# A graph network on one core: the attention's alphas and sums moved from a tail into the second gather pass

## The chip, the core and the metric

The kernel runs on one NeuronCore of a Trainium2 chip. Time is device time of one execution in microseconds (us); a run's time is a little over the span of the profiled instructions. The core has a matrix engine (PE, with its weight loads shown as PEld), a vector engine (DVE), a scalar engine (ACT), GpSimd (POOL), which issues the indirect DMAs, and SyncE (SP), which issues most of the plain ones. Each engine runs its own instructions strictly in the order in which the program emits them, and waits on semaphores for the others.

## The reference, cut to what matters

There are N = 12500 nodes with 256 features, and E = 200000 edges, sorted by `dst`. Two graph convolutions with a residual are followed by one attention layer of H = 4 heads and C = 64 channels.

```python
def _gcn_conv(x, W, b, src, dst, n):
    h = x @ W
    deg = segment_sum(ones, dst)
    dinv = where(deg > 0, rsqrt(deg), 0.0)
    return segment_sum(h[src] * (dinv[src] * dinv[dst])[:, None], dst) + b

def _L1_gnn_ref(x, edge_index, weight, attn_l, attn_r):
    xt = (x @ weight).reshape(-1, heads, out_ch)
    row, col = edge_index
    alpha_l = einsum('ehd,hd->eh', xt[row], attn_l)
    alpha_r = einsum('ehd,hd->eh', xt[col], attn_r)
    alpha = softmax(leaky_relu(alpha_l + alpha_r, 0.01), axis=1)
    tmp = einsum('nh,nhd->nd', alpha[:n], xt[col[:n]])
    return broadcast_to(tmp[:, None, :], (n, heads, out_ch)).reshape(n, -1)

h = relu(layernorm(x));  x = x + gnn(h)        # pre, two _gcn_conv (self loops added), post
h = relu(layernorm(x));  x = x + _L1_gnn_ref(h)
```

Row i of the attention uses edge i, for i < n only. As the edges are sorted by `dst`, the first 12500 edges end in the first few hundred nodes, while their `src` lies anywhere. So edge i needs four numbers of any node (`alpha_l`) and a row of 260 numbers (256 of `xt`, four of `alpha_r`) of an early node.

## The kernel before, in words

**Tiles and chunks.** The nodes are NT = 98 tiles of 128; the edges are NCH = 112 chunks of J = 14 gathers of 128 edges, 1563 gathers in all. Each convolution is a pass over all gathers: POOL fetches the 128 source rows of a gather by an indirect DMA (L1397), DVE makes a chunk's one-hot matrices `fhot` of the edges' places (L1243), and PE multiplies the two and adds up in PSUM (`facc`, L1407). Rows are kept in DRAM as three bf16 parts whose sum is the f32 value, so a gather takes three bf16 matmuls. Rows land in rotating buffers `fgot`; in pass 2 there are 4 buffers of `ONE = 9` gathers.

**Stages.** Preparation; pass 1, whose first 56 gathers take raw rows of x, the next 336 f32 rows of `ftable1`, the remaining 1171 bf16 parts (`split_rows` makes the parts, three gathers apart, while the f32 gathers run); pass 2, 1563 gathers of bf16 parts; and an attention tail.

**The order by hand.** `convolve` emits the whole program for a pass, gather by gather. Work of a finished node tile is queued with `at(t + o, step)` and emitted when the loop has reached gather t + o. A chunk's sums are copied by ACT (`fsums`, L1288), transposed by PE eight gathers later (`fturn`, L1208) and added on DVE thirteen gathers later (`buf`, L1305); the tile that this completes has its steps 6 to 34 gathers on. In pass 2 these are `finish2`'s d (`fpz`), e, f (`fpo`), g (the new x, stored to `kept_x` by SP), h, i (`fpt`), k, q (`fpx`: the product with the attention's weights) and r. A tile completes about every 16 gathers. Before its first gather, `convolve` turns the first rows' own sums (self loops) on PE and calls `ready(0)`.

**What belongs to the attention.** In step r ACT copies tile w's four `alpha_l` numbers and stores them to two tables in DRAM, `table_l` and `table_e`, and for the first XW = 9 tiles the 260-number rows to `table_r`. During pass 2 `set_up` loads `src` and `dst` to all partitions and makes the one-hots `hot_l` and `hot_t`, and the rows of the first 14 edge tiles (`fxe`) are multiplied early. After pass 2 the tail goes through the 98 edge tiles in groups of G = 7. For each tile POOL gathers `alpha_l` by `src` (`fal`, L1751) and PE fetches the end's row by a one-hot product (`fends`, L1741), which ACT copies (`fxg`, L1743). For each group DVE forms the scores, the softmax (with ACT's Exp), the weighted sum over heads (`near`, `far`, `some`, `more`, `fmix`), and adds it to `kept_x` (`fxr`, loaded by SP) to give `fres`, which SP stores. `missing` adds the last three tiles' alphas for the first 14 edge tiles.

**A second path.** If the edges don't fit the kernel's assumptions, a flag `bad` starts a general path after all this; here it is not taken.

Of the kernel before, what the change touches and what calls it, by code (L numbers as in the profile page):

```python
# [8 lines left out]
F32 = mybir.dt.float32  # L9
# [404 lines left out]
def fast_path(  # L414
# [64 lines left out]
    assert AC * J == NT and AC * CE <= E and XW < NT  # L479
    table_r = dram.tile([XW * P, DR], F32, name="table_r")  # L480
    table_l = dram.tile([NT * P, H], F32, name="table_l")

    LW = 3
    table_e = dram.tile([NT * P, H], F32, name="table_e")
# [18 lines left out]
    base_b = const.tile([P, NCH], F32, name="base_b")  # L503
    row_i = const.tile([P, AC], I32, name="row_i")
# [88 lines left out]
    with tc.tile_pool(name="fprep", bufs=1) as prep:  # L593
# [233 lines left out]
        with tc.tile_pool(name="fpsum", bufs=2, space=PSUM) as psum, \  # L827
# [227 lines left out]
            wide = prep.tile([NCH, P], F32, name="wide")  # L1055
            nc.vector.tensor_copy(wide, base.to_broadcast([NCH, P]))
# [7 lines left out]
            nc.tensor.matmul(fk[:, 2, :NCH], wide, ident[:NCH, :NCH], start=True, stop=True)  # L1064
# [7 lines left out]
            for f in after:  # L1072
                f()
            after = [raw_block(ends, m, psum.tile([P, 4 * P], F32, name="ft"), j0)
                     for j0 in (8, 12)]
            nc.vector.tensor_copy(base_b, fk[:, 2, :NCH])
            nc.vector.tensor_scalar(row_i, base_b[:, :AC], lane, float(XW * P - 1), op0=ALU.add,
                                    op1=ALU.min)
# [16 lines left out]
    def check_chunks(work, psum):  # L1095
# [20 lines left out]
        kept = work.tile([1, 1], F32, name="n_kept", bufs=1)  # L1116
        nc.vector.tensor_reduce(kept, pt[:1, 2, :NCH], AX.X, ALU.add)
        nc.vector.tensor_add(kept, kept, counted)
        nc.vector.tensor_scalar(bad_row, kept, -1.0, float(NCH + 1), op0=ALU.mult, op1=ALU.add)
# [12 lines left out]
    def load_late(pool):  # L1132

        nc.scalar.dma_start(roots, root_t)
        for t, w in ((wb, w2), (wo, w_post), (wg[:, :, :D], w_gat)):
            nc.scalar.dma_start(t, w.rearrange("(k p) n -> p k n", p=P))
        nc.scalar.dma_start(b2c, b2.rearrange("(k p) -> p k", p=P))
        nc.scalar.dma_start(bob, b_post.partition_broadcast(P))
        attn = []
        for a in (attn_r, attn_l):  # L1140
            ar = pool.tile([P, D], F32, name="far", bufs=2)
            nc.scalar.dma_start(ar, a.rearrange("h c -> (h c)").partition_broadcast(P))
            attn.append(ar)
        return attn

    def late_weights(pool, attn):

        for i, ar in enumerate(attn):
            for k in range(KC):
                prod = pool.tile([P, H, C], F32, name="fprod", bufs=1)  # L1150
                nc.vector.tensor_mul(prod.rearrange("p h c -> p (h c)"), wg[:, k, :D], ar)
                nc.vector.tensor_reduce(wg[:, k, D + i * H:D + (i + 1) * H], prod, AX.X,
                                        ALU.add)

    def convolve(ep, table, stride, width, ahead, with_sum, psum, prepare, finish, parts, since,
                 lacking=False, raw=(), rows_p=None, behind=None):
# [35 lines left out]

        def new_buf():
# [24 lines left out]
        for n0 in range(0, BW, P):  # L1218
            v, n = {}, min(P, BW - n0)
            new_turned(v)  # L1220
            turn_sums(load_rows(n0, n), 0, v)
            nc.vector.tensor_copy(state["buf"][0][:, :, n0:n0 + n], v["pt"][:, :KC, :n])
            if with_sum:
                nc.vector.tensor_copy(state["buf"][1][:, n0:n0 + n], v["ps"][:, 0, :n])
# [6 lines left out]
        ready(0)  # L1231


        const_p = psum.tile([P, P if with_sum else P + D], F32, name="iota_p", bufs=1)
        iota_p = const_p[:, :P]
        nc.vector.tensor_copy(iota_p, iota_w)
        if not with_sum:
            state["bias"] = const_p[:, P:]
            nc.vector.tensor_copy(state["bias"], bob)

# [21 lines left out]
        def new_rows_of():  # L1262
            if with_sum:
                return new_got()
            return rows_p.tile([P, ONE, 3 * stride], BF16, name="fgot", bufs=ahead)

        def late_sums():
# [3 lines left out]
            froms = new_rows_of().rearrange("p j d -> p (j d)")[:, :J * D]  # L1271
            froms = froms.rearrange("p (j d) -> p j d", d=D)
            assert stride == TW * P and D == TW * P
            for i in range(TW):
                one_hots(froms[:, :, i * P:(i + 1) * P], from_0[:, i, :])
            px = psum.tile([P, KC, P], F32, name="fpt", bufs=1)
# [100 lines left out]
        for t, (c, j) in enumerate(tiles):  # L1377
# [4 lines left out]
            if many == 1:  # L1382
                if j == 0:
                    gots = (raw + [spare])[c] if raw and c <= len(raw) else new_rows_of()
                got = gots[:, j, :]
            else:
                i = (t - since * J) % ONE
                if i == 0:
                    gots = new_rows_of()
                    if since:  # L1390
                        gots = gots.rearrange("p j d -> p (j d)").bitcast(BF16)
                        gots = gots[:, :ONE * 3 * stride].rearrange("p (j d) -> p j d", j=ONE)
                got = gots[:, i, :]
# [16 lines left out]
            if some and j == nj[c] - 1:  # L1410
                for i in range(TW):
                    nc.tensor.matmul(acc, late[0][:, i, :], late[1][i], start=False,
                                     stop=(i == TW - 1))
            if j == nj[c] - 1:
# [3 lines left out]
            if behind:  # L1418
                behind(t)
            run(t)  # L1420
        run()
# [51 lines left out]
    def split_rows(pool, psum):  # L1473
        rows = {}

        def load(w):
            rows[w] = pool.tile([P, D1], F32, name="frow", bufs=4)
            nc.sync.dma_start(rows[w], table1[w * P:(w + 1) * P, :])

        def step(t):  # L1480
# [3 lines left out]
            if k < NT:  # L1484
                load(k)
            if k >= 2:
                p = psum.tile([P, 4, P], F32, name="fpt", bufs=1)
                p = p.rearrange("p a b -> p (a b)")[:, :D1]
                b = pool.tile([P, 3, D1], BF16, name="frow_p", bufs=3)
# [3 lines left out]
                to_parts(p, b, parts1, k - 2)  # L1493

# [5 lines left out]
    assert 3 * D1 * ONE <= 2 * D1 * J and J * D <= 3 * D * ONE  # L1500
# [341 lines left out]
```

## Time and profile before

| | us |
|---|---|
| three runs of the kernel, median | 4876.28 |
| the same, lowest and highest | 4865.6, 4886.07 |
| the profiled execution's own time | 4877.83 |
| its span | 4875.9 |
| preparation, to the first gather from the f32 table's chunks | 0 to 135 |
| pass 1, f32 rows | 135 to 675 |
| pass 1, bf16 parts, with the wait for pass 2's first rows | 675 to 2378 |
| pass 2, first to last gather | 2378 to 4626 |
| what is left of pass 2 after its last gather | 4626 to 4669 |
| the attention's tail | 4669 to 4876 |

The stages are read from the start times of POOL's gathers (L1397 and L1751). POOL is in the row of the gathers' issue nearly all the time: one issue takes 949 ns (2720 of them, 2580.2 us), with 0.30 us between two. DVE and ACT are busy 28% and 13% of the span, PE 54%; the mean granted clock of PE is 0.68 of full speed.

In the tail, POOL's 98 gathers, PE's products, ACT's copies and DVE's mixing follow each other group by group; there is no other work beside them.

### The profile page before, as it was taken

The page shows a single profiled execution, that of the slowest core. Times are in us where ns is not written, and L with a number is a line of the kernel's source. Part 1 is how long each engine was busy: PE and PEld are TensorE (multiplying, and loading weights), DVE is VectorE, ACT ScalarE, POOL GpSimd, SP SyncE. Part 2 cuts the span into 40 slices and gives each one's busy share as a digit, 9 for nine tenths or more (in the row PEclk, how much of TensorE's full clock was granted, in tenths as well). Part 3 has the DMA queues.
Part 4 walks back from the last instruction along what each step waited for, and adds up shares of the span by engine and source line. Part 5 has one row for each costly group of instructions (what it writes and reads, how often), then busy time and mean ns, then how long its engine had stood idle before and what let it go on. Part 6 is the DMA issues. An engine that isn't in the chain of part 4 may idle for free. (4 is left out here: it accounts for less than half of the span.)

```text
span 4875.9 us, 38956 instructions
## 1 busy us (share of the span) xinstructions
PE 2648.6 (54%) x13306; PEld 1780.7 (37%) x13306; DVE 1387.0 (28%) x3009; ACT 614.7 (13%) x1625; POOL 3109.7 (64%) x3299
## 2 busy tenths in 40 slices
PE   5756555555555555555545555545455555545553
PEld 4534433233233333333333334333333343434341
DVE  7445532112122222222222222222222222212236
ACT  5212210000000000000001100010111101101011
POOL 7566646666666666666566666666666666666643
PEclk7766666666666666666666667666676766767766
DMA  8566655555555555555556666565566666656635
GB/s 269 147 178 184 191 157 154 159 158 161 163 156 161 158 162 157 160 157 163 147 157 177 162 159 155 158 161 151 154 159 160 157 156 156 163 153 158 159 110 155
DMA packets 413533, 787.28 MB, mean 161 GB/s; under 512 B 101005, under 2 KB 267172, under 8 KB 413324
## 3 DMA queue, kind: packets, MB, share of 16 engines
q0 software_dynamic: 197264, 594.53, 46.8%
q1 hardware_dynamic: 170214, 173.89, 11.4%
q10 hardware_dynamic: 45846, 16.27, 1.3%
q8 instruction: 107, 1.75, 0.2%
q14 instruction: 102, 0.84, 0.1%
HBM read 692.31 MB, written 92.05 MB: 161 GB/s over the span
## 5 line engine op out<-in xcount | busy, mean ns | idle before, releaser
L1397 POOL DMA_INDIRECT fgot<-parts,fsrc_t x2720 | 2580.2, 949 | 1372.9 <-issue 783.2
L1407 PE MATMUL facc<-fgot,fhot 128*128 128x256 bf16 (+2 forms) x8986 | 1743.4, 335 | 1152.0 <-issue 1105.8
L1407 PEld LDWEIGHTS <-fhot 128*128 128x128 bf16 x8202 | 902.3, 113 | 1593.5 <-issue 1399.0
L1243 DVE TENSOR_TENSOR fhot<-iota_p,to_t 128x1792 bf16<-128x1792 f32 (+1 forms) x224 | 449.2, 2005 | 8.0 <-remote 8.0
L1397 POOL DMA_INDIRECT fgot<-ftable,fsrc_t x336 | 318.8, 949 | 184.0 <-issue 104.2
L1468 DVE TENSOR_TENSOR fpo<-fpo,fparts 128x256 f32<-128x256 f32 x97 | 41.8, 431 | 922.8 <-ACT fo L1454 704.4
L1549 DVE SCALAR_TENSOR_TENSOR fy<-rb,fb2c,fpz 128x128 f32<-128x128 f32 x194 | 58.7, 344 | 850.4 <-remote 677.6
L1305 DVE TENSOR_TENSOR buf<-buf,fturn 128x256 f32 x224 | 94.4, 421 | 699.1 <-remote 510.0
L1558 PE MATMUL fpo<-fwo,fz 128*128 128x256 f32 x388 | 149.2, 523 | 200.1 <-ACT fz L1552 126.8
L1288 ACT ACTIVATE fsums<-facc 128x257 f32<-128x257 f32 (+1 forms) x224 | 85.2, 380 | 1326.9 <-remote 1122.2
L1563 DVE SCALAR_TENSOR_TENSOR fx<-fpo,fdinv,fxb 128x256 f32<-128x256 f32 x97 | 46.9, 483 | 643.4 <-remote 366.9
L1407 PEld LDWEIGHTS facc<-fgot,fhot 128*128 128x128 f32 x784 | 179.4, 237 | 131.2 <-issue 98.1
L1445 PE MATMUL fpo<-wf,buf 128*128 128x256 f32 x388 | 149.2, 496 | 125.5 <-issue 82.3
L1542 PE MATMUL fpz<-buf,fwb 128*128 128x128 f32 x776 | 137.4, 327 | 117.6 <-issue 99.5
L1558 PEld LDWEIGHTS fpo<-fwo,fz 128*128 128x128 f32 x388 | 91.3, 261 | 233.1 <-ACT fz L1552 142.6
L1208 PE MATMUL fturn<-fident,fsums 128*128 128x128 f32 x448 | 118.4, 348 | 100.2 <-issue 52.4
L1542 PEld LDWEIGHTS fpz<-buf,fwb 128*128 128x128 f32 x776 | 121.7, 236 | 127.4 <-issue 104.4
L1208 PE MATMUL fturn<-fident,self 128*128 128x128 f32 x396 | 106.6, 352 | 82.5 <-issue 46.7
L1445 PEld LDWEIGHTS fpo<-wf,buf 128*128 128x128 f32 x388 | 87.9, 248 | 161.5 <-issue 99.1
L1597 PE MATMUL fpx<-fwg,ht 128*128 128x4 f32 (+1 forms) x388 | 69.2, 286 | 129.9 <-ACT ht L1588 99.0
L1751 POOL DMA_INDIRECT fal<-table_l,fsrc_t x84 | 80.5, 958 | 69.3 <-DVE fs L1758 44.6
L1208 PEld LDWEIGHTS fturn<-fident,fsums 128*128 128x128 f32 x448 | 70.7, 177 | 144.8 <-issue 75.4
(284 smaller groups left out, 2272.8 us busy)
## 6 DMA issues: line engine op xcount, KB each, us to landing
fgot<-parts,fsrc_t POOLq DMA_INDIRECT x2720
parts<-frow_p SPq DMA_DIRECT2D x98, 195.0 KB
parts<-fparts SPq DMA_DIRECT2D x98, 192.0 KB
frow<-ftable SPq DMA_DIRECT2D x98, 130.0 KB
self<-ftable SPq DMA_DIRECT2D x99, 128.0 KB
self<-ftable SPq DMA_DIRECT2D x97, 130.0 KB
ftable<-fo ACTq DMA_DIRECT2D x98, 128.0 KB
kept_x<-fx SPq DMA_DIRECT2D x98, 128.0 KB
```

The source lines that it names most:

```text
L1208: nc.tensor.transpose(v["pt"][:, i * KC + k, :], rows[:, k * P:(k + 1) * P], ident)
L1243: nc.vector.tensor_tensor(h, iota_p[:, None, :].to_broadcast([P, n, P]), to[:, :, None].to_broadcast([P, n, P]), ALU.is_equal)
L1288: nc.scalar.activation(sb, acc, AF.Copy)
L1305: nc.vector.tensor_add(b, b, v["pt"][:, :KC, :])
L1397: nc.gpsimd.indirect_dma_start(out=got, out_offset=None, in_=rows_of[:(NT - TW) * P, :] if some else rows_of[:], in_offset=bass.IndirectOf ...
L1407: nc.tensor.matmul(acc, hots[c][:, j, :], got[:, i * stride:i * stride + width], start=(j == 0 and i == 0), stop=(j == nj[c] - 1 and i == ...
L1445: nc.tensor.matmul(po, buf[:, k, :P], wf[:, k, :], start=(k == 0), stop=False)
L1542: nc.tensor.matmul(pz[:, m, :], wb[:, k, m * P:(m + 1) * P], buf[:, k, :P], start=(k == 0), stop=(k == KC - 1))
L1549: nc.vector.scalar_tensor_tensor(y[:, m, :], v["root"], b2c[:, m:m + 1], v["pz"][:, m, :], op0=ALU.mult, op1=ALU.add)
L1558: nc.tensor.matmul(po, v["z"][:, m, :], wo[:, m, :], start=(m == 0), stop=(m == KC - 1))
L1597: nc.tensor.matmul(px, v["ht"][:, k, :], wg[:, k, d0:], start=(k == 0), stop=(k == KC - 1))
L1751: nc.gpsimd.indirect_dma_start(out=al[:, i, :], out_offset=None, in_=(table_l if c else table_e)[:], in_offset=bass.IndirectOffsetOnAxis(a ...
```

## The change

The attention's work is moved into pass 2. `convolve` takes a list `behind` of items. `feed(t)`, called once a gather, takes the first item if its condition holds (so many tiles finished) and the space of the item before has passed, and queues the item's parts one gather apart. The items, in order (the number is the space in gathers):

- `begin`, `picked` (4): small tables.
- `ends_of_tile` (14 times 7): an SP DMA with an address read from memory loads, for each edge tile, the 32 consecutive early nodes that its edges can end in; partition 4n + h holds head h of the n-th of them (65 numbers).
- `alpha_r` (14 groups, 4 each): a row of the edges' ends, broadcast by DMA to all partitions (229 KB, bf16); a one-hot on DVE (128 x 896); 7 f32 products; an ACT copy into `al`.
- `late_hots` (4 times 6) and `late_ends` (16 times 4), for *late* edges, those whose `src` lies in tile LATE = 84 or after: transposed one-hots and rows of 260 numbers, stored to DRAM.
- `alpha_l` for stages of source tiles (0,18), (18,36), (36,54), (54,72): once a stage's tiles are done, the four numbers per node are split into three bf16 parts (`l_of_stage`), and for each of 14 groups (4 gathers each) a row of `src` mod 128 is loaded by SP (229 KB), DVE makes a bf16 one-hot, PE multiplies (21 bf16 products of 72 columns), and DVE masks by the source tile (`mask`), multiplies 128 x 504 in PSUM, reduces, and adds to `al`.
- The last stage (72,84) and the rest are 14 `group` items, 10 gathers apart (the last 17): the `alpha_l` part, the softmax in two parts, the shares split into three bf16 parts, turned by one product, spread over 128 partitions by 7 products (`pick`), multiplied by the one-hot of the ends (`weigh`), and 7 f32 products with `ends` that give the mixed rows. `add_mix` adds them to `kept_x` and stores the group; the last two groups wait in `mixes`.
- `rest` (three): the same sum for the last 14 tiles, once their x is done.

Late edges have a wrong row after this, which is replaced: `list_late`, spread over pass 1, lists up to 16 times 128 late edges with their fields (7 products for each of 14 groups, and small steps). After the last gather, POOL fetches their rows of `kept_x` (16 gathers, 10 of them earlier), PE makes 16 products with the late tiles' alphas, DVE the softmax and the sums, in rounds of 2, 2, 4, 4, 4 of the 16, and POOL scatters the 16 groups of rows to `out`.

Removed are the tail, both alpha tables, `own_rows`, `set_up`, and the early ends. Further: PSUM banks of pass 2 are shared out anew (`fX`, `fY`, two `behind`); gather blocks of pass 2 are 3 buffers of 14 in place of 4 of 9; `frow` and `frow_p` have two buffers each in place of 4 and 3, and the load comes after the use; in pass 1 the first rows' sums (`begin_sums`) and `ready(0)` come after chunk 0's products.

```diff
@@ convolve
+        free_at = [0]
+        def feed(t):
+            if behind and t >= free_at[0] and behind[0][0]():
+                _, space, parts = behind.pop(0)
+                for i, part in enumerate(parts):
+                    if part:
+                        at(t + i, lambda _, part=part: part())
+                free_at[0] = t + space
...
-        ready(0)
+        if not with_sum:
+            begin_sums()
+            ready(0)
...
-            return rows_p.tile([P, ONE, 3 * stride], BF16, name="fgot", bufs=ahead)
+            return rows_p.tile([P, J, 3 * stride], BF16, name="fgot", bufs=ahead)
...
+            if with_sum and t == J - 1:
+                begin_sums()
+                ready(0)
...
-            if behind:
-                behind(t)
+            if every:
+                every(t)
+            feed(t)
             run(t)
@@ finish2, step r
-            nc.scalar.activation(xa[:, d0:], v["px"], AF.Copy)
-            nc.scalar.dma_start(table_l[w * P:(w + 1) * P, :], xa[:, DR:])
-            if w < NT - LW:
-                nc.scalar.dma_start(table_e[w * P:(w + 1) * P, :], xa[:, DR:])
...
+            nc.scalar.activation(l_all[:, w, :], v["px"][:, DR - d0:], AF.Copy)
+            mark("w", w)
@@ attend
+        def alpha_l(s, b):
...
+            def load():
+                v["row"] = row_of(lo_rows, b, "lo_all", 1)
+            def equal():
+                v["h"] = new_hot().bitcast(BF16)[:, :HE]
+                nc.vector.scalar_tensor_tensor(v["h"], v["row"], 0.0,
+                                               banks["lane"].to_broadcast([P, HE]),
+                                               op0=ALU.subtract, op1=ALU.is_equal)
+            def product():
+                p = bank()[:, :G * nw * H]
+                for j in range(G):
+                    for i in range(3):
+                        nc.tensor.matmul(p[:, j * nw * H:(j + 1) * nw * H],
+                                         v["h"][:, j * P:(j + 1) * P], l_parts[s][:, i, :],
+                                         start=(i == 0), stop=(i == 2))
...
+            def taken():
...
+                nc.vector.tensor_tensor(v["p"], v["p"],
+                                        mask[:, :, :, None].to_broadcast([P, G, nw, H]), ALU.mult)
...
+            return [load, None, equal, product, taken]
...
+        def group(b):
...
+            return [load, None, equal, product, taken, lambda: v["soft"][0](),
+                    lambda: v["soft"][1](), split, turn, turned, over(0, 4), weigh(0, 4), over(4, G),
+                    weigh(4, G), mix, end]
@@ after pass 2
-        for g in range(len(groups) + 2):
-            if g < len(groups):
-                keep(g)
-                ends_of(g)
-            if g >= 2:
-                mix(g - 2)
+        for k in range(KL):
+            nc.tensor.matmul(z[k // 8][:, k % 8, :, :], sets["hot"][:, k * P:(k + 1) * P],
+                             l_all[:, LATE:, :], start=True, stop=True)
...
+        for n in [2, 2] + [4] * ((KL - 4) // 4):
...
+            nc.vector.tensor_mul(near, heads[:, k, :, :C],
+                                 share[:, k, :, None].to_broadcast([P, n, H, C]))
...
+            for i in range(k0, k0 + n):
+                nc.gpsimd.indirect_dma_start(
+                    out=out[:], out_offset=bass.IndirectOffsetOnAxis(ap=late_i[:, 0, i:i + 1],
+                                                                     axis=0),
+                    in_=sets["x"][:, i, :], in_offset=None)
```

The emitted order puts the parts of pass 2 here, in gathers of that pass: `alpha_r` 317 to 369, `late_hots` 372 to 390, `late_ends` 396 to 456, `alpha_l` from 463 with four stages of 56 gathers each, the groups 1408 to 1553 of 1563. In pass 1 `list_late` lies between gathers 376 and 490.

## The prediction

> **What bounds the kernel now.** I read the page's totals first, then a table of stages, then the tail's groups, then who waits in pass 2. The totals and the two costliest groups:
>
> ```profile
> PE 2648.6 (54%) x13306; PEld 1780.7 (37%) x13306; DVE 1387.0 (28%) x3009; ACT 614.7 (13%) x1625; POOL 3109.7 (64%) x3299
> ...
> L1397 POOL DMA_INDIRECT fgot<-parts,fsrc_t x2720 | 2580.2, 949 | 1372.9 <-issue 783.2
> L1407 PE MATMUL facc<-fgot,fhot 128*128 128x256 bf16 (+2 forms) x8986 | 1743.4, 335 | 1152.0 <-issue 1105.8
> ```
>
> A gather costs POOL 0.949 us and 0.30 of issue, 1.25. The table of stages (length; busy us and count of PE, PEld, DVE, ACT, POOL; clock; DMA share; GB/s) gives what a gather really takes:
>
> ```profile
> 135.00:231.00 96.00, 66.46 (x280) 51.52 (x281) 45.47 (x146) 30.90 (x66) 53.42 (x56) 0.72 0.46 127
> ...
> 3000.00:3600.00 600.00, 316.75 (x1825) 230.14 (x1825) 136.42 (x295) 62.53 (x172) 392.84 (x415) 0.70 0.60 156
> ...
> 4626.00:4669.00 43.00, 27.39 (x161) 22.12 (x159) 15.62 (x49) 10.82 (x30) 6.20 (x7) 0.81 0.23 65
> 4669.00:4876.00 207.00, 82.24 (x254) 50.13 (x254) 108.12 (x202) 35.45 (x101) 94.18 (x98) 0.62 0.48 148
> ```
>
> Pass 2 takes 600/415 = 1.446 us per gather: 0.19 over POOL's own. The first stage, where PE (69%) and DVE (47%) also work on raw rows, takes 96/56 = 1.714. The last 207 us hold nothing but the attention, with no engine over 52%. Where POOL's 0.19 go shows in its waits from 2378 to 4626 us (total, times, longest):
>
> ```profile
> POOL fgot L1397 <- issue: 445.1, 1460, 0.3
> POOL fgot L1397 <- remote: 245.2, 73, 4.9
> POOL fgot L1397 <- PE facc L1407: 28.9, 7, 7.2
> ```
>
> Some 90 pauses of 2 to 5 us for a buffer that PE must free. So POOL sets the pace, and PE and what PE waits for set its pauses. What PE waits for from 3000 to 3600 us:
>
> ```profile
> PE facc L1407 <- issue: 104.0, 122, 2.5
> PE fpz L1542 <- issue: 38.8, 15, 8.7
> PE fpo L1558 <- ACT fz L1552: 32.0, 7, 10.6
> PE fpx L1597 <- ACT ht L1588: 22.7, 4, 12.7
> ```
>
> When PE does wait at a step between engines, it is long (32.0/7 = 4.6 us), but only in 7 of some 26 tiles.
>
> **What the change removes.** The sum goes against the profiled execution's own 4877.8 us, 1.5 over the median of the runs.
>
> The tail, 4668.5 to 4875.9: -207.4. In its place after the last alpha:
> 16 products. The nearest row is `lacks` on the chain of waits, 42 records in 8.77 us, two records a product, 0.42 each: 6.7. Mask and reduce, four DVE operations of 448 elements by `more` (0.59): 2.4, and 0.2 for an add. Softmax: six small operations at 0.19, and 1.85 for ACT's Exp and back (DVE's idle time before L1763, 27.7 us in 15): 3.0. Three operations over 16 x 256 elements, 12288 in all, by `near`:
>
> ```profile
> L1751 POOL DMA_INDIRECT fal<-table_l,fsrc_t x84 | 80.5, 958 | 69.3 <-DVE fs L1758 44.6 <-issue 24.7
> ...
> L1774 DVE TENSOR_TENSOR near<-fxg,share 128x896 f32<-128x896 f32 (+2 forms) x13 | 13.2, 1015 | 0.4
> ...
> L1779 DVE TENSOR_TENSOR more<-near,far 128x448 f32<-128x448 f32 (+2 forms) x15 | 8.9, 592 | 0.0
> ```
>
> 1.015 us for 896 gives 13.9. The last four scatters: 4 x 1.25 = 5.0, and 5 to land. No scatter is in the trace; by a gather's issue it is 1.25, at most the 2.30 of the raw rows' gathers in preparation, which would make 16 of them 42 us and the tail some 65; at best all hides but the last, 28. I take 36.2. The `rest` items (DVE 1792, 1024 and 768 elements, about 4 us) lie in the 43 us after the last gather, where DVE is busy 15.6; without that cover they cost 4. Net -171.2 (bounds -179 to -142).
>
> Pass 1's start: PE turns self rows from 138.8 to 146.4 while chunk 0's rows wait for it; put behind the products they leave the path, but the one-hots and raw scaling stay. -5 (0 to -7). `own_rows`, `hot_l`, `hot_t` and 14 early products (6.7 us of PE, 24.1 us of idle time before them): -5 (0 to -8). The two stores of alphas per tile were ACT issues off the path: 0.
>
> **What it adds.** An `alpha_l` item, every 4 gathers (5.8 us at the present pace): DVE one-hot of 896 elements by `fhot` (2.02 us for 1792) 1.0, mask 0.2, multiply and reduce of 504 by `more` 0.66 each, add 0.2: 2.7 us, or 47% on top of 23%. PE: 21 products; successive `fpx` records of 4 columns start 0.11 us apart and gathers' of 256 columns 0.11 or 0.21 by the clock, so 2.3 to 4.4 us on top of 53%. That fits only narrowly, and it is of the first stage's kind (DVE 47%, PE 69%, the next matrix waiting for DVE), which pays 1.714 - 1.446 = 0.27 a gather. Below stands 0: gathers in pass 1 and pass 2 keep 1.43 to 1.45 however many tile steps lie among them, since POOL's pauses have room behind them. Queued behind PE's wait for a one-hot are the gathers' products, and behind these the buffer that POOL needs. I take 0.20, nearer the upper row because DVE's share is the higher: 224 x 0.20 = +45 (0 to +60).
>
> The 14 groups, 147 gathers: 10 gathers hold about 43 products and 8 us of DVE of 14.5, with five returns from PE to DVE or ACT. I take the whole 0.27: +40 (0 to +80, twice the row).
>
> `alpha_r` and the late items, 144 gathers with about a quarter of that work: 0.07 each, +10 (0 to +39). `list_late`, 114 gathers in pass 1, 14 times 2 us of DVE and 7 short products: 0.08 each, +9 (0 to +31). The upper ends are 0.27.
>
> SP: 98 broadcasts of 229 KB, 22 MB. The nearest row, `to_all` of 896 KB, was used 6 us after issue at 2494.4; here two gathers (2.9 us) lie between load and use, and four between two uses of the one buffer. DMA is 60% busy, so I take 0; SP's queue also holds `rb`, `fxb` and self loads, needed tiles later. If a load comes 1 us late each time, 56 us; that is in the rival below. Blocks of 14: 42 gathers in flight in place of 36; gain or loss under 20, I take 0.
>
> The Trainium skill speaks against more DVE work beside gathers: SBUF — State Buffer, section "SBUF: two separate sides", says that GpSimd cannot write descriptors while DVE holds the shared port in a two-port mode. The rows do not show it: a gather takes 0.949 us in the mean and 0.958 in the tail with DVE at 52%. If all of some 270 us of added DVE work held the port, the sum would be some 270 higher; by the rows it is not changed.
>
> Sum: 4877.8 - 171.2 - 5 - 5 + 45 + 40 + 10 + 9 = 4800.6; against the median, 4799.
>
> **The rivals.** *The cover holds wholly.* The added work disappears in PE's idle 47% and in POOL's pauses: 4877.8 - 181.2 - 1.5 = 4695. For: the pace of a gather is the same in the f32 stage, pass 1 and pass 2. Against: 0.27 in the first stage.
>
> *Lock-step, slower.* In `alpha_l` DVE's next one-hot stands behind `taken`, which needs PE's product; PE's next product needs that one-hot. If each return takes the 4.6 us of PE's waits for ACT, an item takes 1.7 (mask to add) + 1.0 + 2.3 + 4.6 = 9.6 against 5.8: +3.8 x 56 = 213 in place of 45, so 4967. It decides as soon as the additions pass 181 + 24, that is 1.8 us more per item than I take. For: DVE shows waits for PE of up to 18 us. Against: only 7 of 26 tiles wait, and in the raw chunks four such returns in 14 gathers cost 4 to 6 us.
>
> *The tail does not shrink as said.* The last group ends ten gathers before the end, but PE works up to 36 gathers behind POOL; if the last three groups and the late rows are still due when the gathers stop, each group costs what it cost in the tail (207/14 = 15): 4799 + 45 = 4844.
>
> **How the numbers follow.** Forecast 0.38 (own range 4755 to 4845), wholly covered 0.22, lock-step 0.28, long tail 0.12. About 0.5%, 24 us, is what a measurement of this kernel can tell from no change: same is 4852 to 4901. Faster: 0.35 of the forecast's, 0.22 and 0.06 of the long tail's, 0.63; same: 0.03 + 0.06 + 0.03 of a lock-step in half of the items, 0.12; slower: the rest of the lock-step, 0.25. The range goes from the covered case, less the unknown ends, 4685, to 4960, just short of the full lock-step; 0.07 are left below and 0.13 above.
>
> **What would show it.** Right: the time per gather is 1.6 to 1.75 in the gathers 463 to 519, 641 to 697, 935 to 991, 1229 to 1285 and 1408 to 1553, and 1.45 elsewhere; pauses still end on PE; 75 to 85 us after the last gather. Wrong: 1.45 everywhere (covered); over 2.2 there, with PE waiting for `hot_s` and DVE for `behind` (lock-step); gathers' own duration over 1 us (the port); over 110 us after the last gather (long tail); POOL ending on DMA `lo_all` (the loads).

## The result, and the profile after

The changed kernel takes 5085.66 us (median of four runs, 5071.06 to 5091.46) against 4881.17 for the kernel before (four runs): ratio 1.0418, 95% interval 1.0398 to 1.0437. It is 4.2% slower; 4799 had been forecast. In the last seven runs of this study the kernel before takes 4150 us, also on a chip on which it had taken 4878 earlier; these runs are kept apart below, and the result above belongs to the condition with some 4880.

The page of the changed kernel, the lines that answer to those of before:

```profile
PE 2786.0 (55%) x15210; PEld 1956.4 (39%) x15210; DVE 1627.4 (32%) x3575; ACT 623.8 (12%) x1643; POOL 3029.6 (60%) x3226
...
L1419 POOL DMA_INDIRECT fgot<-parts,fsrc_t x2720 | 2570.9, 945 | 1682.8 <-issue 788.1
L1429 PE MATMUL facc<-fgot,fhot 128*128 128x256 bf16 (+2 forms) x8986 | 1776.6, 343 | 967.6 <-issue 922.5
```

A gather's issue takes as long as before (945 ns, 949 before); POOL's idle time in front of the gathers has grown by 310 us. The stages are read from the starts of POOL's gathers. Pass 2 begins at 2381.2 (2378.6 before), issues its last gather at 4930.7, and the span ends at 5069.3. So pass 2's gathers take 2549.5 us, 302.5 more than before; what lies behind them takes 138.6 in place of 250.4; pass 1 and what lies before it, 2.6 more. The sum, +193.3, is the whole difference of the two spans. Of the 302.5, 13 us lie in the gathers 0 to 310 of the pass, 56 in 310 to 463, 23 in 463 to 530, 128 in 530 to 1405 and 82 in 1405 to 1562. A table of stretches (length; busy us and count of PE, PEld, DVE, ACT, POOL; clock; DMA share; GB/s):

```profile
2837.00:3002.00 165.00, 104.82 (x555) 89.61 (x554) 44.75 (x86) 13.89 (x48) 81.20 (x86) 0.60 0.54 148
...
3410.00:3513.00 103.00, 50.44 (x380) 36.22 (x380) 35.95 (x72) 6.28 (x18) 56.72 (x60) 0.64 0.52 149
3615.00:3744.00 129.00, 66.92 (x373) 49.80 (x371) 25.96 (x59) 12.32 (x34) 85.37 (x92) 0.66 0.54 156
...
4752.00:4931.00 179.00, 106.06 (x736) 86.10 (x735) 89.05 (x211) 28.51 (x60) 77.44 (x83) 0.67 0.67 209
4931.00:5069.00 138.00, 49.79 (x323) 41.37 (x322) 54.15 (x127) 19.13 (x44) 31.29 (x33) 0.67 0.35 105
```

POOL's count tells the pace: `alpha_r` 165/86 = 1.92 us a gather, an `alpha_l` stage 103/60 = 1.72, plain gathers 129/92 = 1.40, the groups 179/83 = 2.16. DMA is busy 67% at most. What POOL waits for in the whole pass (total, times, longest):

```profile
POOL fgot L1419 <- issue: 451.6, 1463, 4.4
POOL fgot L1419 <- PE facc L1429: 450.6, 44, 15.9
POOL fgot L1419 <- remote: 141.9, 46, 5.3
```

By the starts of its gathers POOL pauses 99 times in pass 2 (97 before), but the pauses are twice as long: 597 us beyond the usual 1.25 in place of 291, and those that end on PE's gather products reach 15.9. All 99 stand at the first gather of a block of 14, and 91 of the 97 before at the first of a block of 9: there POOL needs a buffer that PE has to free. One more thing is seen in the timeline of a group (start, length, engine, line, tile, count; in brackets the idle time before and what ended it):

```profile
4947.89 0.70 PE L2066 MATMUL behind<-l_parts,hot_s 128*128 128x48 bf16 x21 [0.66 <-DVE hot_s L2058]
...
4948.76 1.70 PE L2147 MATMUL behind<-ends_all,weights 128*128 128x64 f32 x14
...
4954.33 0.52 DVE L2076 TENSOR_TENSOR behind<-behind,mask 128x336 f32<-128x336 f32 x1 [4.70 <-remote]
...
4961.45 0.54 ACT L2155 ACTIVATE mixes<-behind 128x448 f32<-128x448 f32 x1 [11.86 <-remote]
```

PE's 21 products end at 4948.6 by their records and DVE, idle from 4949.6, starts on them at 4954.3; the mixed rows end at 4950.5 and ACT, idle, starts at 4961.5. POOL issues eleven of the late edges' 16 gathers (not ten, as said of the change) back to back from 4945.7 to 4959.1. In the first case DVE itself is not late: the trace has PE's semaphore rise at 4954.30, 0.03 us before DVE starts. The kernel before shows the same: of 261 instructions of DVE and ACT in pass 2 that wait for PE and stood idle when PE's record of the product ended, half start more than 1.1 us behind that end, a quarter more than 5.7.

After the last gather: 67.9 us until the 16 products with the late alphas begin at 4998.6 (the last groups and tiles), 13.7 to the first scatter, 44.6 for the 16 scatters, and 12.4 to the end.

```profile
5046.71 0.97 POOL L2298 DMA_INDIRECT out_dram<-fgot,late_i  x1 [2.23 <-DMA out_dram<-fgot,late_i]
5049.39 0.97 POOL L2298 DMA_INDIRECT out_dram<-fgot,late_i  x1 [1.71 <-DMA out_dram<-fgot,late_i]
```

Each scatter waits for the landing of the one before.

### The profile page after: what moved, and what is told of

Same layout as the page of the kernel before. It is cut to its first block, busy times and chain, and to the rows that moved or that the text cites. A ratio compares the mean times of both kernels' runs of the same rounds, so it can differ in the third digit from the quotient of the medians.

```text
span 5069.3 us, 43794 instructions
## 1 busy us (share of the span) xinstructions
PE 2786.0 (55%) x15210; PEld 1956.4 (39%) x15210; DVE 1627.4 (32%) x3575; ACT 623.8 (12%) x1643; POOL 3029.6 (60%) x3226
## 5 line engine op out<-in xcount | busy, mean ns | idle before, releaser
L1429 PE MATMUL facc<-fgot,fhot 128*128 128x256 bf16 (+2 forms) x8986 | 1776.6, 343 | 967.6 <-issue 922.5
L1825 PE MATMUL fX<-buf,fwb 128*128 128x128 f32 x776 | 164.3, 361 | 138.6 <-issue 115.6
L1832 DVE SCALAR_TENSOR_TENSOR fy<-rb,fb2c,fX 128x128 f32<-128x128 f32 x194 | 58.6, 344 | 547.3 <-remote 477.3
L1846 DVE SCALAR_TENSOR_TENSOR fx<-fX,fdinv,fxb 128x256 f32<-128x256 f32 x97 | 46.8, 483 | 582.6 <-remote 274.2
L2066 PE MATMUL behind<-l_parts,hot_s 128*128 128x72 bf16 (+1 forms) x1470 | 91.0, 223 | 237.1 <-issue 152.1
L1825 PEld LDWEIGHTS fX<-buf,fwb 128*128 128x128 f32 x776 | 143.7, 268 | 148.1 <-issue 119.8
L1841 PE MATMUL fX<-fwo,fz 128*128 128x256 f32 x388 | 131.2, 471 | 113.1 <-issue 69.4
L2066 PEld LDWEIGHTS <-hot_s 128*128 128x128 bf16 x1470 | 73.6, 116 | 262.8 <-issue 165.1
L1880 PE MATMUL fY<-fwg,ht 128*128 128x4 f32 (+1 forms) x388 | 75.8, 304 | 130.6 <-ACT ht L1872 88.8
L1841 PEld LDWEIGHTS fX<-fwo,fz 128*128 128x128 f32 x388 | 85.3, 244 | 133.2 <-issue 73.3
```

Of the source, the lines that this page charges most:

```text
L1429: nc.tensor.matmul(acc, hots[c][:, j, :], got[:, i * stride:i * stride + width], start=(j == 0 and i == 0), stop=(j == nj[c] - 1 and i == ...
L1825: nc.tensor.matmul(pz[:, m, :], wb[:, k, m * P:(m + 1) * P], buf[:, k, :P], start=(k == 0), stop=(k == KC - 1))
L1832: nc.vector.scalar_tensor_tensor(y[:, m, :], v["root"], b2c[:, m:m + 1], v["pz"][:, m, :], op0=ALU.mult, op1=ALU.add)
L1841: nc.tensor.matmul(po, v["z"][:, m, :], wo[:, m, :], start=(m == 0), stop=(m == KC - 1))
L1880: nc.tensor.matmul(px, v["ht"][:, k, :], wg[:, k, d0:], start=(k == 0), stop=(k == KC - 1))
L2066: nc.tensor.matmul(p[:, j * nw * H:(j + 1) * nw * H], v["h"][:, j * P:(j + 1) * P], l_parts[s][:, i, :], start=(i == 0), stop=(i == 2))
```

## The experiments

Runs are single unless said otherwise, each with the kernel before on the same chip; one run is good to some 0.3%. The changed kernel by its ratio would take 5103 us beside a before of 4898.7, and 5080 to 5082 beside 4876 to 4878.

**Is it the round trip?** Three edits to the `alpha_l` items, and one that stretches the groups.

```diff
# no_alpha_l: the four stages' items left out
-                items.append((when("w", STAGES[s][1]), 4, alpha_l(s, b)))
# no_return: products made, never read
+                items.append((when("w", STAGES[s][1]), 4, alpha_l(s, b)[:4]))
# late_taken: `taken` three gathers later, behind the next item's one-hot
-            return [load, None, equal, product, taken]
+            return [load, None, equal, product, None, None, None, taken]
# groups_wide: two gathers between steps that wait for another engine
-            return [load, None, equal, product, taken, ...
+            return [load, None, both, product, None, None, None, taken, ...
```

> The 56 alpha_l items of the first four stages are left out (their alphas are missing in the result). By the trace of the changed kernel the gathers in and just behind these four windows take some 150 us more than 1.44 us each. Both theories expect a time 130 to 165 us under the changed kernel's 5086, so 4920 to 4955; a time above 5000 would say that the loss in these windows is only moved to another place.

> The alpha_l items keep their row load, one-hot and 21 products, but no one reads the products (the three DVE operations and the add of `taken` are left out). Round-trip theory (DVE's next one-hot stands behind `taken`, which waits for PE's result to be noticed, and PE stands until that one-hot): 100 to 140 us gained, 4945 to 4985. Work theory (the added products, one-hots and loads cost this much in any order): 50 us or less gained, above 5035.

> All work is kept; only `taken` of an alpha_l item is emitted seven gathers after the load in place of four, so the next item's one-hot no longer stands behind it. Round-trip theory: 70 to 120 us gained, 4965 to 5015, and an item takes 6 to 6.5 us in place of 8.3. Work theory: no change beyond 20 us, 5065 to 5105.

> All work is kept; the steps of a last-stage group stand two gathers apart where one engine waits for another (25 gathers long in place of 15, still 10 between groups). In the changed kernel a group takes 22 us where 10 gathers should take 14.4. Round-trip theory: 40 to 80 us gained in the gathers, 10 to 20 lost after the last gather, so 5010 to 5060. Work theory: nothing gained, 5085 to 5110.

Beside 4898.7 us: no_alpha_l 5017.6, no_return 5102.3, late_taken 5095.2, groups_wide 5116.0. The items cost 86 us, less than the 128 that the trace shows in the gathers 530 to 1405, and less than the 130 to 165 expected: by the expectation's own mark of 5000, part of the loss is elsewhere. In that run the gathers 530 to 1405, with no item among them, still take 38 us more than in the kernel before, 5 of them by that chip's 0.4% alone; what makes the rest was not tested. Without any reader of the products all of the 86 is still there, and with the one-hots freed from `taken` all but 8. So for these items my round-trip theory, the lock-step of the prediction, falls: DVE's waits for PE are real, and cost at most 8 us here. With groups_wide the gathers 1450 to 1562 take 223 us in place of 241 to 248, 13 are lost after the last gather (151.7 against 138.6), and the whole run is 13 us slower. So the groups' spacing is worth some 20 us in the gathers, and nothing in all.

**Which ingredient is it?** The `alpha_l` items were replaced by windows with one or two ingredients each, mostly on constant operands and with no readers.

```diff
-            for b in range(NG):
-                items.append((when("w", STAGES[s][1]), 4, alpha_l(s, b)))
+        def many(n, cols, hot=None):
+            def f():
+                p = bank()
+                for i in range(n):
+                    nc.tensor.matmul(p[:, (i % 7) * cols:(i % 7 + 1) * cols],
+                                     (held["h"][:3 * QP, (i % 7) * P:(i % 7 + 1) * P] if hot
+                                      else ident_b[:3 * QP, :]),
+                                     pick[:, i % 7, :cols], start=True, stop=True)
...
+        for kind, w in zip(kinds_in_order, range(30, 80, 7)):
+            for b in range(NG):
+                items.append((when("w", w), 4, kinds[kind]))
```

> The four stages' alpha_l items are left out, and in their place stand eight windows of 14 items, 4 gathers apart, from tiles 30, 37, 44, 51, 58, 65, 72 and 79 (about gathers 541, 653, 765, 877, 989, 1101, 1213, 1325 of pass 2), each with one ingredient; read is the extra time of POOL's gathers in a window and 60 gathers behind it against the run without alpha_l items. In order: 21 products of 72 columns with constant operands; 42 of them; 7 of them; the 224 KB row load alone; the one-hot alone; one-hot and 21 products of it; 21 products and a DVE reduce of the result; 21 products of 8 columns. PE-instruction theory (while POOL issues gathers PE gets through its instructions slowly, so each added product costs, whatever its size): 25 to 35 us for each window of 21, 55 to 75 for 42, 5 to 12 for 7, under 6 for load and one-hot alone, and the same 25 to 35 for 8 columns. Load theory (the broadcasts hold up the gathers): 20 to 30 in the load's window, under 10 elsewhere. DVE theory (the one-hot delays the next matrix): 20 to 30 in both one-hot windows, under 10 where only PE works.

> As the other probe, with another order, so that a window's place can be told from what is in it: load, one-hot and 21 products together; one-hot alone; 21 products of 8 columns; 21 of 72 columns; 42; the load alone; 7; one-hot and 21 products. PE-instruction theory: 25 to 40, under 6, 25 to 35, 25 to 35, 55 to 75, under 6, 5 to 12, 25 to 35. Load theory: 20 to 30 in the first and sixth, under 10 elsewhere. DVE theory: 20 to 30 in the first, second and last.

They took 5085.8 and 5083.7 us beside 4877.7. From the starts of POOL's gathers, the length of 112 gathers from 530, 642, 754, 866, 978, 1090 and 1202 on, and of 91 from 1314 on, less the same gathers of the kernel before (us; 14 items each):

```
probe_a  21 products 16.4 | 42 products 32.6 | 7 products 11.0 | row load 3.2
         one-hot 1.2 | one-hot + 21 26.7 | 21 + DVE reduce 25.5 | 21 of 8 columns 23.1
probe_b  load + one-hot + 21 20.7 | one-hot 5.2 | 21 of 8 columns 20.5 | 21 products 25.5
         42 products 38.9 | row load (behind the 42) 12.3 | 7 products 3.8 | one-hot + 21 17.3
```

With no item at all (no_alpha_l) the same windows stand 1.6 to 6.9 us above the kernel before, 4.8 in the mean, so loads and one-hots cost nearly nothing; the load's 12.3 in probe_b follows the 42 products. The windows with 14 times 21 products take 16 to 27 us, 22.0 in the mean of eight, whether somebody reads the products or not, and eight columns as much as 72: less the 4.8, some 0.06 us for each of 294 products. So it is PE's added work, as the work theory said; most sizes lie below its 25 to 35. These windows do not tell PE's time from PE's instructions: each product has the same weight load, and a record lasts 168 ns at 8 columns and 214 at 72.

**Does less PE work help, and do SP's loads matter?**

```diff
# one_stage: one stage of 72 source tiles, 294 products of 288 columns
-    STAGES = [(0, 18), (18, 36), (36, 54), (54, 72), (72, 84)]
+    STAGES = [(0, 72), (72, 84)]
# light_apart: alpha_r's row six gathers ahead, late_ends every 8 gathers
-            return [load, None, equal, product, taken]
+            return [load, None, None, None, None, None, equal, product, taken]
-            items.append((when("w", XW), 4, late_ends(k)))
+            items.append((when("w", XW), 8, late_ends(k)))
# one_light: both
```

> The four stages of alpha_l become one of 72 source tiles: 14 items in place of 56, the same sums, with 294 products of 288 columns in place of 1176 of 72, and 98 returns of one bank each in place of 56. PE-instruction theory, at the 0.05 to 0.07 us that a product cost in the probes: 44 to 62 us gained, ratio to before 1.029 to 1.033 in place of 1.042. Round-trip theory (a return costs, whatever it carries): nothing gained or some us lost. Column theory (PE's time counts, 85 thousand columns in all before and after): nothing gained.

> The alpha_r items load their row six gathers before its use in place of two, and late_ends stand eight gathers apart in place of four; all work is kept. Gathers 310 to 530 of pass 2 take 395 us in the changed kernel, 315 before. If SP's late loads and the few buffers are the cost there, 30 to 50 us of these 80 come back and the ratio falls to 1.032 to 1.036. If PE's added instructions are (some 290 records, 20 us), at most 10 us come back in all.

> Both edits before together. If they are separate costs the gains add: ratio to before 1.020 to 1.028. Neither theory expects it to come under the kernel before, since the groups (80 us) and the tail are untouched.

Beside 4876.3 us: 5040.9, 5081.9 and 5040.4. Taking out 882 products gains some 40 us, 0.045 each, just under the 44 to 62 expected, although the number of returns has grown from 56 to 98 and the columns are the same. The edit also takes out 42 one-hots and 42 row loads, which by the probes cost nearly nothing; so it speaks for PE's number of products and against returns and columns. In light_apart nothing came back in all. (The gathers 310 to 530 take 371 us in place of 395, but the first 23 us of `alpha_l` have moved out of them.)

What `alpha_r` and the late items cost, 49 us in the gathers 310 to 420 of the changed kernel, stands beside 36 us of PE records of `alpha_r`'s f32 products (196 records), but no edit in this condition shows that these are the cause. The trace shows a rival in SP's queue, which light_apart leaves in place. The 98 loads of `ends_of_tile` occupy SP until 2903.8, gather 350, and the loads behind them come late (the changed kernel; SP, PE, DVE and POOL together):

```profile
2854.53 21.28 SPq L1960 DMA_DIRECT2D ends_all<-table_r  x14
...
2876.86 0.37 SPq L1223 DMA_DIRECT2D self<-ftable  x1
2880.01 0.69 PE L1229 MATMUL fturn<-fident,self 128*128 128x128 f32 x2 [18.73 <-DMA self<-ftable]
2886.21 0.94 POOL L1419 DMA_INDIRECT fgot<-parts,fsrc_t  x1 [14.28 <-PE facc L1429]
...
2903.84 1.43 SPq L1943 DMA_DIRECT2D rel_all<-rel_rows  x2
2906.14 1.09 DVE L1949 SCALAR_TENSOR_TENSOR hot_s<-rel_all,iota_p 128x896 f32<-128x896 bf16 x1 [16.20 <-DMA rel_all<-rel_rows]
2907.38 3.15 PE L2029 MATMUL behind<-right,hot_s 128*128 128x4 f32 x14 [11.04 <-DVE right L2023]
2918.95 0.94 POOL L1419 DMA_INDIRECT fgot<-parts,fsrc_t  x1 [15.56 <-PE facc L1429]
```

PE stands 18.7 us for a self load and 11.0 for the first `alpha_r`, and after each POOL makes one of its two longest pauses there. light_apart has the same wait for the self load, 18.3 us. How much of the 49 us this is was not tested.

**Who paces the pass?** In the kernel before, one memset more on POOL for each gather of pass 2.

```diff
+            if not with_sum:
+                nc.gpsimd.memset(idle_p, 0.0)
```

> The kernel before with one small POOL memset behind every gather of pass 2, which holds POOL for about 0.25 us more, 1.50 in place of 1.25 a gather. If PE paces the pass and POOL's pauses are slack, the pauses go and the pass takes 1.50 to 1.53 a gather: 95 to 150 us longer, ratio 1.02 to 1.03. If POOL's issue and a fixed pause for each block set the pace, all is added: 350 to 400 us, ratio above 1.07.

4893.5 us beside 4876.3, less than either theory expected, but the edit does not load POOL: the memset (117 ns) fits into the 0.30 us between two gathers.

```profile
2384.03 0.10 POOL L1404 MEMSET idle_p<- 128x1 f32 x1 [5.95 <-DMA parts<-fparts]
...
2999.97 0.95 POOL L1398 DMA_INDIRECT fgot<-parts,fsrc_t  x1 [0.19 <-issue]
3000.92 0.11 POOL L1404 MEMSET idle_p<- 128x1 f32 x1
3001.23 0.95 POOL L1398 DMA_INDIRECT fgot<-parts,fsrc_t  x1 [0.19 <-issue]
```

Where POOL doesn't pause, gathers start 1.251 us apart, 1.254 in the kernel before. The first memset waits once, 5.95 us, for a DMA; that makes the first 42 gathers 6.4 us longer. So this run says nothing on who paces the pass.

The traces say more. From 3000 to 3600 us of the kernel before PE stands still for 104.0 us before gather products with nothing that the profile shows to wait for (`PE facc L1407 <- issue`, in the prediction's table). Here is the stretch before one of POOL's pauses (3032.74 to 3036.07):

```profile
3027.87 0.37 PE L1407 MATMUL facc<-fgot,fhot 128*128 128x256 bf16 x1 [1.82 <-issue]
3028.59 0.38 PE L1407 MATMUL facc<-fgot,fhot 128*128 128x256 bf16 x1 [0.34 <-issue]
3029.30 0.37 PE L1407 MATMUL facc<-fgot,fhot 128*128 128x256 bf16 x1 [0.33 <-issue]
3031.40 0.37 PE L1407 MATMUL facc<-fgot,fhot 128*128 128x256 bf16 x1 [1.73 <-issue]
...
3037.03 1.44 PE L1407 MATMUL facc<-fgot,fhot 128*128 128x256 bf16 x6
```

The second and third product of a gather wait for no semaphore. In pass 2 of the kernel before they start 0.27 us behind the one before in the mean, and 369 of 3095 more than 0.4 behind it, most of these some 0.70, 1.40 or 2.10. In the 10 us behind a pause of POOL that is 2% of them, later 49%. In alpha_r_bf16 below, where POOL makes no such pauses, none of 3055 is over 0.4, and the mean is 0.15. So PE itself stops while POOL issues, catches up behind a pause, and frees the buffers for which POOL waits. That PE's pace sets the pass's is read from these traces, and from the probes' unread products, which lengthen it; the edits that were to show it in the kernel before did not (this one, and two_parts below).

**The scatters.**

```diff
-                    out=out[:], out_offset=bass.IndirectOffsetOnAxis(ap=late_i[:, 0, i:i + 1],
+                    out=aside[i][:], out_offset=bass.IndirectOffsetOnAxis(ap=late_i[:, 0, i:i + 1],
```

> The 16 scatters go to 16 scratch tables in place of one output, so none waits for the one before (the late rows are missing in the result). In the changed kernel they are issued 2.7 to 3.2 us apart, 44.6 us from first to last. If each waits for the landing of the one before, they now follow DVE's rounds: first to last 15 to 20 us, and 24 to 30 us gained in all. If POOL's own work makes the 2.8 us, nothing is gained.

5068.5 us beside 4877.7. First to last scatter 19.8 us in place of 43.6, and 114.2 us after the last gather in place of 138.6. The chain is the wait for the landing, and costs 24 us there. The whole run is only 13 us under the changed kernel's 5082, as pass 2's gathers took 17 us longer in it, within what one run is good to.

**The other condition.** The next runs were meant to tell PE's time from its count of instructions and to show the kernel before with less PE work.

```diff
# two_parts (kernel before, pass 2): the third part's product left out
-            for i in range(many):
+            used = many if with_sum else many - 1
+            for i in range(used):
# alpha_r_bf16: one-hot in bf16, three exact parts
-                    nc.tensor.matmul(v["p"][:, j, :], v["h"][:, j * P:(j + 1) * P],
-                                     v["r"][:, j, :], start=True, stop=True)
+                    for i in range(3):
+                        nc.tensor.matmul(v["p"][:, j, :], v["h"][:, j * P:(j + 1) * P],
+                                         v["b"][:, i, j, :], start=(i == 0), stop=(i == 2))
# probe_c: windows with f32 products, 512 columns, chains over ACT and DVE
# one_bf16: one_stage and alpha_r_bf16 together
```

> The kernel before; in pass 2 each gather has two products in place of three (the rows' third bf16 part is fetched and left out of the sum). Nothing else changes: the same gathers, bytes, DVE and ACT work. If PE paces the pass, its 1563 fewer products of 256 columns (0.11 to 0.21 us each) bring the gathers from 1.44 us towards POOL's own 1.25: 110 to 250 us gained, ratio 0.95 to 0.977. If POOL's issue and fixed pauses pace it, nothing is gained.

> The changed kernel with alpha_r's 7 f32 products of an item (14 records, whose weight loads and products fill PE for some 2.6 us) replaced by 21 bf16 products of three exact parts (about 1.1 to 1.5 us of PE), and four small DVE operations more. Theory of PE time: gathers 310 to 420 of pass 2, 205 us in the changed kernel and 156 before, come down by 15 to 30. Theory of PE's instruction count: 21 in place of 14, so they grow by about 5.

> Windows of 14 items, 4 gathers apart, in place of the alpha_l items, at about gathers 541, 653, 765, 877, 989, 1101, 1213, 1325. In order: 7 f32 products of 4 columns (14 records); 7 bf16 products of 512 columns; 14 f32 products; nothing; three PE products chained over two ACT copies, one gather between each; the same over DVE; 21 bf16 products of 72 columns; 7 f32 products again. Theory of PE time (0.19 us a f32 record as in alpha_r, 0.21 to 0.43 for 512 columns, 0.06 to 0.1 for 72): 30 to 40, 15 to 40, 60 to 80, 0, then for the chains only what PE stands still, and 16 to 27 for the 21. Theory of the instruction count: 15 to 20, 5 to 8, 30 to 40, 0, 2 to 4, 2 to 4, 16 to 27. Round-trip cost is what the chains show beyond 4 us: if a return costs 0.5 us, 14 each.

> The kernel before without the third part's products in pass 2, once more: the first run fell on a chip on which the kernel before takes 4151 us and POOL never pauses, so that nothing was there to gain. On a chip where the kernel before takes some 4880 us and PE paces: 110 to 250 us gained. Where POOL paces: nothing.

> The third probe once more, for the same reason. On a chip with some 4880 us before, theory of PE time: 30 to 40 us for 7 f32 products of 4 columns, 15 to 40 for 7 of 512 columns, 60 to 80 for 14 f32, 0 for nothing, 16 to 27 for 21 of 72 columns; theory of the instruction count: 15 to 20, 5 to 8, 30 to 40, 0, 16 to 27. The two chains: 2 to 4 if returns cost nothing, 14 for each 0.5 us of a return.

> alpha_r in bf16 parts once more. On a chip with some 4880 us before: gathers 310 to 420 of pass 2 take 15 to 30 us less than the changed kernel's 205 by the theory of PE time, some 5 more by the instruction count. On a chip with some 4150 before: ratio 0.993, as before.

> Both edits that took PE work out: alpha_l in one stage of 72 tiles, and alpha_r in bf16 parts. On a chip with some 4880 us before, the gains add: ratio 1.025 to 1.031, still slower than the kernel before. On a chip with some 4150 before, PE keeps up anyway and the ratio stays at 0.99 to 0.995.

Beside 4151.3: two_parts 4155.3, alpha_r_bf16 4123.4, probe_c 4134.1. Beside 4149.6: 4158.4, 4123.2, 4137.6, and one_bf16 4152.0. None of the expected losses and gains in the gathers is there, because PE keeps up: POOL issues nearly all gathers 1.25 us apart, with the attention beside it or without. The waits of POOL in two_parts from 2100 to 3900 us, and then a group of alpha_r_bf16:

```profile
POOL fgot L1397 <- issue: 421.1, 1382, 0.3
POOL fgot L1397 <- DMA fgot<-parts,fsrc_t: 9.4, 31, 0.3
POOL fgot L1397 <- PE facc L1408: 3.1, 10, 0.3
```

```profile
3863.86 0.70 PE L2073 MATMUL behind<-l_parts,hot_s 128*128 128x48 bf16 x21 [0.55 <-DVE hot_s L2065]
...
3864.60 0.52 DVE L2083 TENSOR_TENSOR behind<-behind,mask 128x336 f32<-128x336 f32 x1
3864.73 1.67 PE L2154 MATMUL behind<-ends_all,weights 128*128 128x64 f32 x14
...
3866.44 2.02 DVE L2093 TENSOR_TENSOR fxr<-fxr,behind 128x1792 f32<-128x1792 f32 x1 [0.56 <-PE behind L2154]
```

No wait in these rows is longer than a usual issue, and PE's results are taken up at once; in two_parts, 463 starts of DVE and ACT, chosen as above, all lie within 0.1 us of PE's recorded end, where the median was 1.1. In this condition the moved attention is covered nearly whole: alpha_r_bf16 takes 1961.8 us for pass 2's gathers against 1956.8 of two_parts, and 127.9 after them against 163. It is some 27 us, 0.65%, faster than the kernel before, in two runs. That is the only version with all of the work that came under the kernel before, and only there; in the condition of the result it wasn't run, nor was the change itself in this one. one_bf16 gains nothing over the kernel before, against the 0.99 to 0.995 expected: its single stage costs 23 us in the gathers 1300 to 1400. What makes the two conditions differ was not found. It is not the chip, as one chip showed both, and not PE's mean granted clock alone, which is 0.682 in the kernel before and in two_parts.

## Why the prediction was wrong

**Pass 1 and its start: right.** -5 and +9 were forecast; the first gather of chunk 4 comes 2.7 us earlier and pass 2 starts 2.6 later, so list_late and its neighbours cost 5.3.

**The tail: a term mis-sized.** 79 us were forecast after the last gather (43 and 36.2), 138.6 were measured. The scatters were priced at 5 and 5 for landing, as issues one behind the other; they wait for each other's landing and take 44.6. Of the rest, the drain of tiles and last groups is 68 in place of 43: the long-tail rival, at about the half of its price. The products, softmax and rounds behave as priced.

**What was added: the step that failed.** The prediction lets POOL's pauses and PE's idle 47% cover most of the added work, and prices a product by starts 0.11 or 0.21 us apart. Its own table held the row against that, `PE facc L1407 <- issue: 104.0, 122`, the largest of PE's waits, and passed it over: PE stands still between products that wait for nothing, they follow each other 0.27 us apart in the mean, and POOL pauses because PE is behind. So the idle time was not free. What the runs showed in its place: in this condition products that nobody reads and that wait for no other engine's work cost the pass some 0.06 us each. +45, +40 and +10 became 86 (56 `alpha_l` items, by removal, 0.38 a gather), 82 (the gathers 1405 to 1562, over 0.5 a gather) and 78 (the gathers 310 to 530 of no_alpha_l against the kernel before). All three lie above the ranges' upper ends of 60, 80 and 39, so the nearest row, 0.27 in the raw chunks, was no bound. The 0.20 was chosen by DVE's share, and DVE's one-hots cost nothing. No edit showed what the 82 and the 78 are made of; by the trace SP's queue, a term put at 0, has a part in the 78. Some 33 to 38 us more lie in gathers with no item (no_alpha_l), and their cause is open; the only term for such gathers, blocks of 14, was put at 0, under 20.

**The signs.** 1.6 to 1.75 us a gather was to be seen in five windows and 1.45 elsewhere. It is 1.87, 1.60, 1.61, 1.65 and 1.95 there, and 1.56 to 1.58 between the first four.

**The lock-step rival: the right side, the wrong mechanism.** It gave 4967, still 119 us short, and rests on DVE's one-hot behind `taken`. no_return and late_taken take that dependency away and gain 1 and 8 us.

**The row loads and the port: as forecast.** Row loads cost nothing (3 us in probe_a); of SP's loads it is those of `ends_of_tile`, which the prediction doesn't name, that hold others up. The gather's issue stayed at 945 ns with DVE 50% busy in the groups, and at 945 to 949 in every run, so the Trainium skill's rule on the shared port (SBUF — State Buffer, "SBUF: two separate sides") did not show itself in any run here. Whether any of the added DVE work runs in a two-port mode the traces don't say.

**The covered rival** describes the other condition well, and the condition of the measurement not at all.

## What to carry to other kernels

When an engine pauses regularly for buffers, look at the engine that frees them before calling the pauses room. If that one has much idle time ended by nothing that the profile shows, its idle share is no cover; products that nobody reads, put in its way, price it before the work is moved. In this condition hidden matrix work was priced by the number of products more than by their columns, and fewer, wider ones gained 40 us; in the other one_bf16 with its wider ones was 29 us slower than alpha_r_bf16_2 beside it. A probe that is to load an engine must be seen to lengthen that engine's own rhythm: one memset a gather did not. Loads added to a queue also cost what stands behind them in it. A scatter to one tensor is priced by its landing, not by its issue.

## What the hardware showed unasked

In one condition PE's results were taken up 0.04 us after their recorded end and POOL's gathers ran at 1.25 us nearly without pauses. In the other, half of these starts came more than 1.1 us late and one in twenty more than 16, with gathers at 1.44, and the same kernel took 4876 in place of 4150 us. There PE stops between products that wait for nothing, often for 0.70 us or a multiple of it, while POOL issues indirect DMAs back to back; in the 10 us behind a pause of POOL it hardly does, and the products start 0.11 or 0.21 us apart. In the first condition it never does. Why POOL's issuing and PE's stops go together was not found. The sign of this change hangs on it: +4.2% in the one, and, for the version with `alpha_r` in bf16, -0.65% in the other.
